# Loads and stores of a first block: where residual rows, quarters of a weight and split weight terms stand in one DMA queue

## The chip, the cores and the metric

The kernel runs on one core of a Trainium2 chip, as one launch. The metric is the device time of that launch in microseconds (us); lower is better.

## The reference

The input x has shape (4, 1024, 512), in float32. Two branches start from the same layer norm of x, and both are added to x:

```python
xn = layernorm(x)                                   # over the last axis, 512 wide

# time mix: 512 -> 704 -> 512
xx = concat([xn[:, 1:2], xn[:, :-1]], axis=1) - xn  # the row before, minus this row
k = (xn + xx * time_mix_k) @ Wk.T                   # (b, t, 704)
r = (xn + xx * time_mix_r) @ Wr.T
w = exp(-exp(time_decay))
state = state * w + relu(k_t)                       # a scan over t
a = layernorm((state * r) @ Wv.T) * ln_gamma + ln_beta

# FFN: 512 -> 2048 -> 512, rounded to float16 at three places
X = xn.astype(float16)
D = gelu(X @ W0.T + bias0).astype(float16)
E = (D @ W1.T + bias1).astype(float16)

out = x + a + E
```

## The kernel before

**Tiles.** The 4096 rows of x are worked in 8 blocks of 512 tokens (`TB`). A block is computed with channels on the partitions: 512 channels are 4 tiles of 128 (`NC`, index c), the 704 hidden units of the time mix are 5 full tiles and a half one (index h), the 2048 of the FFN are 16 tiles (`NN`, index n), and the 512 tokens of an output are 4 tiles of 128 (`NS`, index s). Index i is the block in the FFN, j = i + 1 the block whose time mix is under way, j2 = i + 2 the block whose rows are being fetched and normalized.

**Split weights.** Matmuls work on pairs of float32r tiles that sum to the float32 value. `split(hi, lo, raw)` makes such a pair: ACT casts the raw tile to the upper part (L165), then DVE subtracts to get the lower (L166). W0 comes in four quarters, *groups* g = 0 to 3, each of 512 hidden units, which serve the four chunks n = 4g to 4g + 3. A group is four raw tiles `w0raw_{g}_{c}` of 256 KB (loaded at L173), whose pairs `w0h`, `w0l` stay for the whole kernel. W1 is split chunk by chunk in block 0 (`w1raw_{n}`, loaded at L182; `w1_0_{n}` has two buffers), the pair is stored in DRAM as `w1d_{n}` (L193, 512 KB), and later blocks load it from there. The weights of k and r are split into three terms each (`split_kr`, tiles `wt_...`, six buffers under the tag `kr`), which are stored as `krd_...` (L223, three stores of 256 KB) for later blocks. Other parts of weights and inputs share a pool of 48 buffers.

**The chunk loop.** Before the loop, block 0's time mix projections are computed, groups 0 and 1 of W0 are loaded and split, chunks 0 and 1 of `up` are issued, and block 1's rows are loaded, normalized and transposed (`transposed`, 16 instructions of DVE at L284). Then each block runs 16 chunks. In chunk n, PE does

- `up(i, n + 2)`: 8 matmuls into a bank `pd` (L650), two for each c; ACT follows with gelu (L660, tile `d16`) and a copy to float32r (L665, tile `d`);
- `down(n)`: 8 matmuls that add to the four banks `pe` (L672), from `d` and the pair of W1;
- a *piece* of the time mix: for n = 0 to 3 `out_piece`, one s of the product with Wv (L578 and, at n = 1 and 3, L590), followed on DVE by a layer norm and by the addition of the residual rows (`residual`, L604, L610, L611); later pieces are the projections of block j.

What lies beside this is put into the lists `bg[n]` by `put(n, ...)` and issued at the end of chunk n: the mixing of block j's inputs (`mixed`), splits, the load of block j2's rows (`fetch_x`), its statistics and its transposes, and the load of the residual rows (`fetch_res`).

**Order.** Inside the loop the order on PE and on the DMA queue of SP is the order of the program (`manual_schedule`); ACT, DVE and POOL are ordered by a planner, which places each instruction by estimated costs and due times. Before the loop the planner orders SP too. Every engine and queue works in its order, so a DMA that has to wait for its source or its buffer holds up those behind it. All of the DMAs named here are issued on SP.

**Buffers that matter here.** A block's rows `x_{i}` and its residual rows `xres_{i}` are tiles of the tag "x", which has one buffer (`load_x`, four DMAs of 256 KB at L100). So `xres_0` can be fetched only after the last transpose of `x_1`, and `x_2` only after the last use of `xres_0`.

Of the kernel before, what the change touches and what calls it, by code (L numbers as in the profile page):

```python
# [11 lines left out]
F32 = mybir.dt.float32  # L12
# [10 lines left out]
def time_mix_and_gelu_ffn(  # L23
# [26 lines left out]
    nc = tc.nc  # L50
# [5 lines left out]
    NC = C // P  # L56
# [21 lines left out]
    def part(name, dtype=F32R, tag="q", bufs=48):  # L78
        return wide.tile([P, TB], dtype, tag=tag, name=name, bufs=bufs)
# [10 lines left out]
    def tokens_of(i, s):  # L90
        b, t0 = blocks[i]
        return b, slice(t0 + s * P, t0 + (s + 1) * P)

    def load_x(i, name, amid=lambda: None):
        xs = const.tile([P, NS, C], F32, tag="x", name=f"{name}_{i}")
        for s in range(NS):
            if s == NS // 2:
                amid()
            b, rows = tokens_of(i, s)
            nc.sync.dma_start(xs[:, s, :], x[b, rows, :])  # L100
        return xs
# [62 lines left out]
    def split(hi, lo, raw):  # L164
        nc.scalar.copy(hi, raw)  # L165
        nc.vector.tensor_sub(lo, raw, hi.bitcast(F32))  # L166

    G = TB // P
    w0 = {}

    def load_w0(g, c):
        raw = part(f"w0raw_{g}_{c}", F32)
        nc.sync.dma_start(raw, w0T[c * P : (c + 1) * P, g * TB : (g + 1) * TB])  # L173
        w0[c, g] = part(f"w0h_{c}_{g}"), part(f"w0l_{c}_{g}")
        split(*w0[c, g], raw)

    w1_dram = [dram.tile([P, 2, C], F32R, name=f"w1d_{n}") for n in range(NN)]
    w1_raw = {}

    def load_w1_raw(n):  # L180
        w1_raw[n] = part(f"w1raw_{n}", F32)
# [2 lines left out]
    def load_w1(i, n):  # L184
        if i == LAST and n >= NN - 2:
            parts = [part(f"w1_{i}_{n}_{p}") for p in range(2)]
            for p in range(2):
                nc.sync.dma_start(parts[p].bitcast(F32), w1_dram[n][:, p, :].bitcast(F32))
            return parts
        w1 = wide.tile([P, 2, C], F32R, tag="w1", name=f"w1_{i}_{n}", bufs=2)  # L190
        if i == 0:
            split(w1[:, 0, :], w1[:, 1, :], w1_raw.pop(n))
            nc.sync.dma_start(w1_dram[n].bitcast(F32), w1.bitcast(F32))  # L193
        else:
            nc.sync.dma_start(w1.bitcast(F32), w1_dram[n].bitcast(F32))
        return [w1[:, p, :] for p in range(2)]
# [15 lines left out]
    def split_kr(kind, h):  # L212
        raw = raw_w.pop((kind, h)).rearrange("p c k -> p (c k)")
        name = f"{kind}_{h}"
        u = truncated(raw, f"wu_{name}")
        d = temp(f"wd_{name}")
        nc.vector.tensor_sub(d, raw, u)
        terms = [part(f"wt_{name}_{p}", tag="kr", bufs=6) for p in range(3)]
        nc.scalar.copy(terms[0], u)
        nc.scalar.activation(terms[1], d, AF.Copy, scale=S)  # L220
        nc.vector.scalar_tensor_tensor(terms[2], d, -S, u, ALU.mult, ALU.add)
        for p in range(3):
            nc.sync.dma_start(kr_dram[kind, h][p].bitcast(F32), terms[p].bitcast(F32))  # L223

    def split_half():
        u = truncated(raw_half.rearrange("p two c k -> p (two c k)"), "half_u")
# [52 lines left out]
    def transposed(xn, first=0, end=(P // Q) ** 2):  # L279
        src = xn.rearrange("p s (c i a) -> p s c i a", c=NC, a=Q)  # L280
        dst = xnT[:, :, 1:].rearrange("p c (s j b) -> p s c j b", s=NS, b=Q)
        for k in range(first, end):
            j, i = divmod(k, P // Q)
            nc.vector.transpose(  # L284
                dst[i * Q : (i + 1) * Q, :, :, j, :],
                src[j * Q : (j + 1) * Q, :, :, i, :],
            )
# [285 lines left out]
    pos, zs, xres = {}, {}, {}  # L573
# [127 lines left out]
    for g in range(2):  # L701
        for c in range(NC):
            load_w0(g, c)
    for n in range(AHEAD):
        load_w1_raw(n)
    load_late_constants()
# [2 lines left out]
    norm_stats(1, x_now)  # L709
    norm_apply(1, x_now)  # L710
    transposed(x_now)
    behind.close()
    xres[0] = load_x(0, "xres")
    for n in range(AHEAD, AHEAD + 2):
        load_w1_raw(n)

# [2 lines left out]
    with tc.manual_schedule(engines={nc.tensor.engine, nc.sync.engine}):  # L719
        for i in range(len(blocks)):  # L720
            j, j2 = i + 1, i + 2
            tail = 4 if i == LAST else 0
            by_columns = range(NS // 2, NS) if tail else ()
            pieces, bg, pre = {}, defaultdict(list), defaultdict(list)

            def put(n, fn, *args):
                bg[n].append(lambda: fn(*args))

            for s in range(NS):
                pieces[s] = [out_piece, i, s]  # L730
            if j <= LAST:
                if i == 0:
                    order = [(0, h) for h in range(NF)] + [(1, h) for h in range(NF)]
                    for k, (kind, h) in enumerate(order):
                        pieces[4 + k + kind] = [(raw_k, raw_r)[kind], j, h]
                        put(5 + k, split_kr, kind, h)
                    pieces[9] = [
                        lambda j: raw_halves(j, [bank(f"pkr_{j}_{q}") for q in range(2)]), j
                    ]
                    put(13, split_half)  # L740
                    for c in range(NC):
                        put(c, mixed, j, c)
                        put(c, load_w0, 2, c)
                        put(6 + c, load_w0, 3, c)
                else:
                    order = [(0, h) for h in range(NF)] + [(1, h) for h in range(NF)]
                    for k, (kind, h) in enumerate(order):
                        pieces[4 + k + 2 * kind] = [three_pass, j, kind, h]

                        def fetch(kind, h):  # L750
                            ks[j, kind, h] = load_kr(j, kind, h)

                        put((2, 3)[k] if k < 2 else 2 + k + 2 * (k > 6), fetch, kind, h)
                    pieces[9] = [half_pass, j, 0]
                    pieces[10] = [half_pass, j, 1]
                    for c in range(1, NC):
                        put(c - 1, mixed, j, c)
                    put(4, split_xr, j, 0)
                    put(8, split_xr, j, 1)
                    put(9, split_xr, j, 2)  # L760
                    put(9, split_xr, j, 3)
            if j2 <= LAST:

                def fetch_x():
                    state["x"] = load_x(j2, "x")

                put(5, fetch_x)
                put(6, lambda: norm_stats(j2, state["x"]))
                put(7, lambda: norm_apply(j2, state["x"]))
                for n, ks_ in enumerate((0, 5, 10, 16)[:-1]):  # L770
                    end = (5, 10, 16)[n]
                    put((8 if i == 0 else 10) + n, lambda a, b: transposed(state["x"], a, b), ks_, end)
                put(13, mixed, j2, 0)
            if j <= LAST:

                def fetch_res():
                    xres[j] = load_x(j, "xres")

                put(14, fetch_res)

            pe = [ps_e.tile([P, C], F32, tag="pe", name=f"pe_{i}_{s}") for s in range(NS)]
            for n in range(NN):
                ahead = n + AHEAD
                if ahead == NN and j <= LAST:
                    xf = ffn_input(j)
                nxt = (i, ahead) if ahead < NN else (j, ahead - NN)
                gelu = up(*nxt) if nxt[0] <= LAST else None
                for follow in followers:
                    follow()
                followers = []  # L790
                if gelu:
                    d = gelu()
                if n == 0:
                    for s, e16 in enumerate(e16s):
                        finish(i - 1, s, e16)
                    e16s = []
                if n < NN - tail:
                    operands = waiting.pop(0)
                    for s in range(NS):
                        down(n, s, *operands, end=NN - tail if s in by_columns else NN)  # L800
                if gelu:
                    waiting.append((d, load_w1(*nxt)))
                if n in pieces:
                    fn, *args = pieces[n]
                    followers.append(fn(*args))
                if i == 0 and n + 4 < NN:
                    load_w1_raw(n + 4)
                for fn in bg[n]:
                    fn()
            if not tail:  # L810
                e16s = [rounded(i, s, pe[s]) for s in range(NS)]

# [56 lines left out]
```

## Time and profile before

| what | value |
|---|---|
| time, median of 3 runs | 931.48 us (931.17 to 932.77) |
| profiled execution, device time | 930.21 us |
| profiled execution, span of the trace | 928.1 us |
| mean granted TensorE clock in it | 0.989 |
| PE busy | 900.6 us (97% of the span) |
| DVE busy | 569.4 us (61%) |
| ACT busy | 340.6 us (37%) |
| POOL busy | 64.2 us (7%) |
| DMA, mean rate | 174 GB/s, 161.66 MB |

The profile records one execution. Its span runs from the first instruction to the last, and 2.1 us of its device time lie outside. Busy time is summed over an engine's instructions. In the timeline a row gives the start, the length, the engine (SPq is the queue of SP in the act of issuing DMAs), the line of the program, the operation, what it writes and reads, and in brackets the idle time ahead of it and what ended that. In the waits a row gives the instruction that waited, what released it, and then the total in us, the number of times and the longest. In the windows a row gives the stretch and its length, then the busy us of PE, PE's weight loads, DVE, ACT and POOL with the number of instructions, then the granted clock of PE as a share of full speed, the busy share of the DMA engines and the GB/s they moved.

Block 0 takes the first part of the span: its chunk loop begins at about 67 us, and the chunk n = 10 lies at about 142 to 160 us.

### The profile page before, as it was taken

Reading aid. Unit: us, or ns where it says so; the run is one execution under the profiler, and the core shown is the slowest. Engines: PE = TensorE matmul, PEld = TensorE weight load, DVE = VectorE, ACT = ScalarE, POOL = GpSimd, SP = SyncE. Lnnn points to the kernel's source line nnn. Section 1 sums busy time; section 2 is a strip of 40 time slices with the busy share of each in tenths; the row PEclk is TensorE's granted clock in tenths of the full one; section 3 lists DMA queues with packets and bytes.
Section 4 is the critical chain, followed back from the end, with each engine's and each line's share of the span. In section 5 each row is a group of like instructions: output and inputs, shape, how many; then the busy total and the mean of one; then the engine's idle time right before and its main releaser. Section 6 shows DMA issues by size and latency. Waiting matters only on the chain.

```text
span 928.1 us, 10514 instructions
## 1 busy us (share of the span) xinstructions
PE 900.6 (97%) x3664; PEld 651.4 (70%) x3664; DVE 569.4 (61%) x954; ACT 340.6 (37%) x578; POOL 64.2 (7%) x142
## 2 busy tenths in 40 slices
PE   8959995999999999999999999999999999999997
PEld 8435663665888668885788758886688857887586
DVE  5975588763586845966478735868459674423223
ACT  4442353531345223442345313442244523442132
POOL 1200000001100010001110001001100000000000
PEclk9989997999999999999999999999999999999999
DMA  9333374563646347462565536463474735655134
GB/s 264 133 125 134 124 253 159 216 227 135 229 153 230 114 168 242 157 228 102 178 231 167 185 136 217 157 223 129 156 245 151 241 103 168 196 161 190 69 116 156
DMA packets 75727, 161.66 MB, mean 174 GB/s; under 512 B 8959, under 2 KB 15132, under 8 KB 75676
## 3 DMA queue, kind: packets, MB, share of 16 engines
q1 hardware_dynamic: 75616, 160.99, 51.7%
q8 instruction: 29, 0.48, 0.2%
q14 instruction: 22, 0.18, 0.1%
q10 hardware_dynamic: 60, 0.02, 0.0%
HBM read 136.33 MB, written 24.64 MB: 173 GB/s over the span
## 4 chain that ended last, share of the span: by engine, by line
PE 91%; DVE 3%; DMA 2%; issue 1%; SPq 1%; ACT 1%; POOL 0%; DVEq 0%; ACTq 0%
PE pe L672 24%; PE pd L650 24%; PE po L578 15%; PE pa L524 12%; PE pb L325 6%; PE pr L325 3%; PE pk L325 2%; PE ph L552 2%; PE po L590 2%; DVE xnT L284 1%; DMA w0raw<-in_L_ffn_W 1%; PE idle L343 1%; DMA w<-w1d 1%; DMA x<-in_L_attn_x 0%; PE end L672 0%
## 5 line engine op out<-in xcount | busy, mean ns | idle before, releaser
L672 PE MATMUL pe<-w,d 128*128 128x512 f32 x1008 | 252.9, 393 | 11.4 <-ACT d L665 10.2
L672 PEld LDWEIGHTS pe<-w,d 128*128 128x128 f32 x1008 | 191.1, 190 | 53.1 <-ACT d L665 11.8
L650 PE MATMUL pd<-xf,w0h 128*128 128x512 f32 x512 | 212.5, 415 | 7.1 <-ACT w0h L165 7.1
L650 PE MATMUL pd<-xf,w0l 128*128 128x512 f32 x512 | 200.4, 391 | 2.4 <-DVE w0l L166 2.4
L660 ACT ACTIVATE d<-pd,late_sb 128x512 f16<-128x512 f32 x128 | 87.8, 686 | 268.1 <-PE pd L650 267.8
L578 PE MATMUL po<-wv_sb,g 128*128 128x512 f32 x320 | 142.6, 592 | 0.0
L650 PEld LDWEIGHTS pd<-xf,w0h 128*128 128x128 f32 x512 | 96.3, 188 | 47.5 <-issue 19.9
L650 PEld LDWEIGHTS pd<-xf,w0l 128*128 128x128 f32 x512 | 96.3, 188 | 28.0 <-issue 6.2
L578 PEld LDWEIGHTS po<-wv_sb,g 128*128 128x128 f32 x320 | 60.9, 190 | 63.8 <-issue 60.6
L260 DVE BATCH_NORM_STATS2 sty<-po 128x6 f32<-128x512 f32 x32 | 21.9, 683 | 124.4 <-PE po L590 124.4
L537 DVE SCALAR_TENSOR_TENSOR y<-pb,a 128x512 f32<-128x512 f32 x60 | 41.3, 689 | 91.8 <-PE pb L325 91.3
L665 ACT CAST d<-d 128x512 fp32r<-128x512 f16 x128 | 79.3, 620 | 3.6
L284 DVE STREAM_TRANSPOSE xnT<-x 32x512 f32<-32x512 f32 x112 | 78.7, 702 | 2.0
L536 ACT ACTIVATE a<-pa 128x512 f32<-128x512 f32 x60 | 35.9, 599 | 114.7 <-PE pa L524 114.7
L524 PE MATMUL pa<-hk,kr 128*128 128x512 f32 x120 | 46.7, 389 | 0.0
L524 PE MATMUL pa<-lk,kr 128*128 128x512 f32 x120 | 46.7, 389 | 0.0
L524 PE MATMUL pa<-hr,kr 128*128 128x512 f32 x120 | 46.7, 389 | 0.0
L524 PE MATMUL pa<-lr,kr 128*128 128x512 f32 x120 | 46.7, 389 | 0.0
L254 POOL TENSOR_SCALAR ry<-mvy 128x1 f32<-128x1 f32 x32 | 15.6, 487 | 423.8 <-DVE mvy L261 423.8
L325 PE MATMUL pk<-xk,wk 128*128 128x128 f32 (+1 forms) x152 | 38.6, 410 | 0.0
L325 PE MATMUL pr<-xr,wr 128*128 128x512 f32 x80 | 35.6, 592 | 0.0
L539 ACT ACTIVATE y<-y 128x512 f32<-128x512 f32 x30 | 19.0, 633 | 43.9 <-DVE y L537 43.9
(130 smaller groups left out, 1001.4 us busy)
## 6 DMA issues: line engine op xcount, KB each, us to landing
w<-w1d SPq DMA_DIRECT2D x110, 512.0 KB, 3.3
kr<-krd SPq DMA_DIRECT2D x180, 256.0 KB, 4.0
x<-in_L_attn_x SPq DMA_DIRECT2D x32, 256.0 KB, 5.0
xres<-in_L_attn_x SPq DMA_DIRECT2D x32, 256.0 KB, 4.4
w1d<-w SPq DMA_DIRECT2D x16, 512.0 KB, 2.9
krd<-wt SPq DMA_DIRECT2D x30, 256.0 KB, 3.6
out<-z SPq DMA_DIRECT2D x28, 256.0 KB, 2.5
w0raw<-in_L_ffn_W SPq DMA_DIRECT2D x16, 256.0 KB, 4.6
```

Source lines behind the costliest of these rows:

```text
L260: nc.vector.bn_stats(st6, src)
L284: nc.vector.transpose(dst[i * Q : (i + 1) * Q, :, :, j, :], src[j * Q : (j + 1) * Q, :, :, i, :],)
L325: return nc.tensor.matmul(dst, w[:, c, :], src, start=(c == 0), stop=(c == NC - 1))
L524: nc.tensor.matmul(pa, w[p][:, c, :], xs[j, c][p], start=(c == 0 and p == 0), stop=(c == NC - 1 and p == 1),)
L536: nc.scalar.activation(a, pa, AF.Copy, scale=1.0 + 1.0 / S)
L537: nc.vector.scalar_tensor_tensor(y, pb, -1.0 / S, a, ALU.mult, ALU.add)
L539: nc.scalar.activation(y, y, AF.Relu)
L578: nc.tensor.matmul(pos[s], gs[i, h][:, s * P : (s + 1) * P], wv_sb[:, h, :], start=(h == 0), stop=False,)
L650: nc.tensor.matmul(pd, w0[c, g][p][:, k * P : (k + 1) * P], xf[c], start=(c == 0 and p == 0), stop=(c == NC - 1 and p == 1),)
L660: nc.scalar.activation(d16, pd, AF.Gelu, bias=b0_sb[:, n : n + 1])
L665: nc.scalar.copy(d, d16)
L672: nc.tensor.matmul(pe[s] if sum_ is None else sum_, d[:, s * P : (s + 1) * P], w1[p][:, cols], start=(n == first and p == 0), stop=(n == e ...
```

## The change

Four things change, all of them in what runs before block 0's loop or within its 16 chunks; the blocks after it run the same instructions.

1. `xres[0] = load_x(0, "xres")` moves from before the loop into `bg[0]`, the end of chunk 0.
2. Group 2 of W0 (the third quarter) is loaded and split before the loop, right behind block 1's transposes in the program, rather than in chunks 0 to 3.
3. `load_w0` is divided into the load and `split_w0`. For group 3 (the last quarter), the loads go to the ends of chunks 4 to 7 and take buffers of the tag `kr`, which the terms of k and r use as well; the splits stay in chunks 6 to 9.
4. The stores of W1's pairs and of the terms of k and r are put in a list when their data is made, and `store_weights()` issues them at the end of the chunk, behind the loads that the chunk issues.

```diff
-    def load_w0(g, c):
-        raw = part(f"w0raw_{g}_{c}", F32)
+    w0_raw = {}
+
+    def load_w0(g, c, **home):
+        w0_raw[c, g] = raw = part(f"w0raw_{g}_{c}", F32, **home)
         nc.sync.dma_start(raw, w0T[c * P : (c + 1) * P, g * TB : (g + 1) * TB])
+
+    def split_w0(g, c):
         w0[c, g] = part(f"w0h_{c}_{g}"), part(f"w0l_{c}_{g}")
-        split(*w0[c, g], raw)
+        split(*w0[c, g], w0_raw.pop((c, g)))
...
+    stores = []
+
+    def store_weights():
+        while stores:
+            nc.sync.dma_start(*stores.pop(0))
...
             split(w1[:, 0, :], w1[:, 1, :], w1_raw.pop(n))
-            nc.sync.dma_start(w1_dram[n].bitcast(F32), w1.bitcast(F32))
+            stores.append((w1_dram[n].bitcast(F32), w1.bitcast(F32)))
...
         for p in range(3):
-            nc.sync.dma_start(kr_dram[kind, h][p].bitcast(F32), terms[p].bitcast(F32))
+            stores.append((kr_dram[kind, h][p].bitcast(F32), terms[p].bitcast(F32)))
...
     for g in range(2):
         for c in range(NC):
             load_w0(g, c)
+            split_w0(g, c)
...
     transposed(x_now)
+    for c in range(NC):
+        load_w0(2, c)
+        split_w0(2, c)
     behind.close()
-    xres[0] = load_x(0, "xres")
...
+            if i == 0:
+
+                def first_res():
+                    xres[0] = load_x(0, "xres")
+
+                put(0, first_res)
...
                     for c in range(NC):
                         put(c, mixed, j, c)
-                        put(c, load_w0, 2, c)
-                        put(6 + c, load_w0, 3, c)
+                        put(4 + c, partial(load_w0, tag="kr", bufs=6), 3, c)
+                        put(6 + c, split_w0, 3, c)
...
                 for fn in bg[n]:
                     fn()
+                store_weights()
```

## The prediction

> **What bounds the kernel now.** I read the page's busy shares first (PE 97% busy, 900.6 of 928.1 us), then the waits of PE, then the timeline of its two long waits, then the windows for the clock. PE lacks 27.5 us, and three waits hold most of it:
>
> ```profile
> PE pe L672 <- ACT d L665: 10.2, 1, 10.2
> PE pd L650 <- ACT w0h L165: 7.1, 2, 6.0
> PE pd L650 <- DVE w0l L166: 2.4, 1, 2.4
> ```
>
> All three lie in block 0, which the change edits. The others are under 2 us each.
>
> **Stall 1, 57.27 to 67.47.** The timeline shows a chain that starts on the SP queue:
>
> ```profile
> 54.78 1.28 SPq L100 DMA_DIRECT2D xres<-in_L_attn_x  x3
> 56.10 0.43 SPq L173 DMA_DIRECT2D w0raw<-in_L_ffn_W  x1
> 61.28 0.62 ACT L165 CAST w0h<-w0raw 128x512 fp32r<-128x512 f32 x1 [3.74 <-DMA w0raw<-in_L_ffn_W]
> 65.71 0.69 ACT L660 ACTIVATE d<-pd,late_sb 128x512 f16<-128x512 f32 x1
> 67.47 3.78 PE L672 MATMUL pe<-w,d 128*128 128x512 f32 x8 [10.21 <-ACT d L665]
> ```
>
> xres_0 shares its one buffer with x_1, so SP holds it until x_1's last transpose (L284) at 54.75. The last load of group 1, w0raw_1_3, stands behind it. ACT works in order: its cast of that tile waits 3.74 us, and kr, relu, the gelu table, gelu and d follow, 6.2 us of mere succession up to the first down().
>
> **Stall 2, about 146 to 158**, inside up(0,12), the first product with group 3:
>
> ```profile
> 148.28 0.32 SPq L193 DMA_DIRECT2D w1d<-w  x1
> 149.01 0.69 DVE L166 TENSOR_TENSOR w0l<-w0raw,w0h 128x512 fp32r<-128x512 f32 x1
> 149.12 1.87 SPq L223 DMA_DIRECT2D krd<-wt  x3
> 151.10 0.66 SPq L173 DMA_DIRECT2D w0raw<-in_L_ffn_W  x1
> 155.76 0.62 ACT L165 CAST w0h<-w0raw 128x512 fp32r<-128x512 f32 x1 [2.19 <-DMA w0raw<-in_L_ffn_W]
> 156.43 0.80 PE L650 MATMUL pd<-xf,w0h 128*128 128x512 f32 x1 [5.96 <-ACT w0h L165]
> ```
>
> The last raw tile stands on SP behind a store waiting for DVE's lower part of w1_0_11 (ends 148.25) and behind three krd stores: issued 151.1, landed 155.7. Undisturbed, up(0,12) would end at 146.33; it ends at 157.95: 11.6 us lost, the waits of 1.16, 2.4 and 6.0 and matmuls at half clock between.
>
> **Clock.** In the windows (busy us by engine, PEclk, DMA share, GB/s), what follows each stall still runs at half rate:
>
> ```profile
> 61.13:67.40 6.27, 0.00 (x0) 0.00 (x0) 4.62 (x8) 5.22 (x8) 0.57 (x1) 0.50 0.35 135
> 67.40:71.37 3.97, 3.90 (x9) 3.13 (x10) 2.41 (x5) 2.09 (x5) 0.00 (x0) 0.50 0.65 264
> 156.40:160.12 3.72, 3.69 (x8) 2.67 (x9) 3.65 (x7) 2.63 (x5) 0.00 (x0) 0.50 0.00 0
> 130.00:152.00 22.00, 16.93 (x79) 9.53 (x77) 21.34 (x33) 8.46 (x15) 0.06 (x1) 0.95 0.63 210
> ```
>
> Half rate costs 1.95 us in the first (3.9 of work at half) and 1.07 in the second (a down() of 2.89 instead of 1.82). The last row counts later: ahead of stall 2 DVE is 97% busy. Losses in all: 10.2 + 1.95 + 11.6 + 1.07 = 24.8 us.
>
> **The Trainium skill.** "TensorE: Matmul & The Clock Gate", Part 1, What's actually happening: after at least one idle window of about 3.4 us the array runs at half clock, and at full after a busy one; the window runs freely. The trace agrees: half from 61.13, 3.86 us after the last matmul, to 71.37, 3.90 after the first. The same page, Architectural detail: ACT and DVE are strict FIFO; here ACT stood 3.74 us at a cast while its next input was ready. "DMA: Bandwidth & Descriptors", Anatomy of one DMA: a semaphore wait is taken on the issuing sequencer, not by the DMA engines; here w0raw_1_3 issued only after xres had its buffer.
>
> **The change part by part.** The counts of PE and POOL instructions stay, and all weight transfers stay on SP.
>
> *xres_0 moved into chunk 0.* SP is idle from 28.1, so w0raw_1_3 issues at once there and lands long before its cast. That goes from 61.28 to about 57.5, where ACT comes from the previous cast: the 3.74 us go, nothing else of the chain. First down() at 67.47 - 3.74 = 63.73, a gap of 6.46, still long enough for half clock; the 1.95 stay, with 0.15 added for the different place in a window: 2.1. xres_0's four DMAs then pass through SP at 59 to 61, landing by 65 (4.4 us to landing on the page); their first reader (L611) comes after 84, so they cost nothing. Without that 19 us the cost would be the chain itself. Gain 3.74 - 0.15 = **3.6**.
>
> *Group 2 ahead of the FFN.* Its four loads, 1 MB, fall into 28 to 54, where DMA is 21% busy (1% in 40 to 50). Four casts of 0.62 and four subtractions of 0.69 move from chunks 0 to 3 to ACT's and DVE's order before, between and after the transposes of x_1. DVE was the busier one, 25.8 of 28 us in 26:54, so they partly fill the gap and can push. They were in chunks where up(0,8) is still 30 us off. Bounds: -0.5 (less crowding in chunk 1) to +2.8 (four DVE splits all before d_0_0). I take 0: the cast that gates gelu hangs on w0raw_1_3, and DVE's share in the gap was 4.62 of 6.27 with slack between.
>
> *What becomes late next.* In the changed kernel's instruction order on ACT, the cast of w1_0_2 no longer comes right after the first down() (71.29 before) but after d_0_4, and DVE's lower part behind z work of the first pair (L604, L610, L611). PE, from 63.73: down 3.7 at half clock, po_0 4.5, up 1.84, down 1.82, po_1 with its halves 5.3, up(0,4) to about 82.95. Then gelu at 83.04, d 83.76, w1's cast 84.28 to 84.90, lower part 85.66 to 86.34, so that the second matmul of down(2) starts at 86.4 rather than 83.2: **3.2 lost** (2.4 if the subtraction goes first, 4.0 if one more z operation precedes it). ACT then waits at w1_0_4 for the landing of w1_0_2's store (about 89.5); the next gelu's input is there only at 94, so this is hidden by 4 us.
>
> *Group 3 two chunks ahead in kr's buffers.* Loads 0 and 1 go at 98 to 111; load 2 must wait until a krd store has landed (about 120), load 3 until a subtraction frees its buffer (130 to 133). It lands by 138, 17 us earlier than now. Stall 2 so loses its DMA part, and what remains is DVE: x_2's load is issued at about 110 rather than 116.85, as it stands behind less on SP, its sixteen transposes of 0.70 end about 5 us earlier, and the last subtraction w0l_3_3 lands at 148.4 to 149.3 (behind the terms of kr_0_4 and w1_0_11) instead of 157.1. With PE arriving 0.5 earlier, up(0,12) would end at 145.8 and ends at 149.0: **3.2 lost** instead of 11.6, and the 1.07 of half clock goes if PE is not idle for a whole window.
>
> The casts of terms borrow from the same six buffers, so ACT may wait for stores: 3.6 us to landing plus 0.6 each for issue. A gelu has about 7 us (one chunk) before down() needs it, so this is 0 while the wait is under that; bounds 0 to 2 per chunk in chunks 6 to 12.
>
> *Stores behind loads.* Same 46 stores, moved back within their chunk by at most a w1 load, four x loads and a w0 load (0.4, 2.3 and 0.7 us of issue). Their readers come only in block 1, over 50 us later. Waiting at the end rather than in the middle, they hold up the next chunk's loads alone, which are two to four chunks early. Zero; bounds -0.5 to +0.5.
>
> Sum: losses after 6.46 + 2.1 + 3.2 + 3.2 = 15.0, so 24.8 - 15.0 = **9.8 us gained**, without new half clock. Both short gaps are just under or about a window with one or two matmuls inside. Before stall 2 a window with roughly 0.5 us of PE work out of 3.4 dropped the clock, one with 2.7 did not; where the limit lies between is not shown. A drop costs 1.7 (half of a window) to 2.5; one in the first gap is passed on, since DVE's later work hangs on PE's through z and the terms. The profiled execution of 930.21 would become 920.4 without a drop; it lies 1.27 below the median of 931.48, so against the median 921.7, with one drop about 923.9, with two 926.2.
>
> **Rivals.**
> 1. *Both gaps drop the clock*: gain 5.3, 926. For: the gaps are as long as a window. Against: matmuls in them.
> 2. *DVE holds stall 2 as it is.* If x_2's transposes aren't earlier, DVE, 97% busy until 152, gives w0l_3_3 at about 153 (the present 157.1 less the 4 that its own load no longer costs), half clock again: up(0,12) ends at 153.7 instead of 157.95, and 4.2 is the whole gain: 927.3.
> 3. *Slower: kr's six buffers.* If terms wait for landed stores in each chunk from 6 to 12, ACT stands 3.6 + 0.6 us while holding the next gelu; where that exceeds the chunk's slack by 1.8 in seven chunks, 12.6 are lost, total 934. It decides once the sum passes 9.8. For: w0raw_3 takes up to four of six. Against: ACT is 37% busy, and a term's chunk is 7.1 us long.
> 4. *The change doesn't do what it says*: the load of group 1 still waits for another buffer. Up to 190 us SP waits only for the subtraction (L193) and for x's buffer (L100), which speaks against it; then stall 1 stays, and 9.8 - 3.6 = 6.2 is left: 925.3.
>
> **Numbers.** Short stalls with at most one drop: 0.62, 921.7 to 923.9; I predict 923.5, nearer the one drop, which I hold for likelier than none. Two drops (rival 1) 0.15; rival 2: 0.09; rival 4: 0.03; slower 0.08; losses that happen to cancel 0.03. Low end 919 from the lower bounds (2.4, one gap less); high end 929 takes in rivals 1, 2 and 4. 0.2% (1.9 us) is about what can be told from no change here.
>
> **What would show it.** Right: w0raw_1_3 issued near 28; first down() near 63.7; a new wait of 1 to 3 us of L672 on w1's cast or subtraction near 83 to 86; w0raw_3_3 issued before 135; the longest wait of L650 under 4 us near 146. Wrong: any wait above 4 us in chunks 5 to 12, ACT idle on krd landings with PE idle beside it, or stall 1 still near 10 us.

## The result, and the profile after

Over seven runs the changed kernel took 925.10 us (923.71 to 928.82), the kernel before 931.53, 6.4 us more. The ratio of the means is 0.9937, with a 95% interval of 0.9919 to 0.9955. The profiled execution was the slowest of the seven, 928.82 us with a span of 926.9, so I read a second trace of the same kernel beside it (label after_again: 924.44 us, span 922.6).

In the code of the changed kernel the lines of the loop stand nine further down: `up` is L659, `down` L681, gelu L669, the copy to d L674, the transposes L293. The waits of PE in the first trace (total, times, longest):

```profile
PE pe L681 <- ACT d L674: 6.5, 1, 6.5
PE small L409 <- issue: 3.1, 1, 3.1
PE pd L659 <- ACT w0h L165: 2.4, 1, 2.4
PE pe L681 <- ACT w L165: 2.0, 1, 2.0
PE pd L659 <- DVE w0l L166: 1.5, 1, 1.5
PE pe L681 <- DVE w L166: 1.0, 1, 1.0
```

The first wait was 10.2. The second belongs to the start of the kernel (2.0 before, so that the prediction's "under 2 us each" for the other waits is just off). The third and fifth together were 9.5, and the two on `w`, 3.0 in all, are new: they stand at `down(2)`. The page's line of busy times,

```profile
PE 904.3 (98%) x3664; PEld 653.3 (70%) x3664; DVE 569.0 (61%) x954; ACT 339.3 (37%) x578; POOL 65.6 (7%) x142
```

shows PE busier than before by 3.7 us with the same 3664 matmuls. That is no extra work: matmuls at half clock last longer, and this execution had more of them. Its windows, in the same columns as before:

```profile
6.00:9.00 3.00, 0.20 (x1) 0.13 (x1) 0.43 (x3) 0.54 (x3) 0.00 (x0) 1.00 0.67 227
9.00:16.00 7.00, 6.87 (x31) 6.28 (x32) 3.55 (x15) 3.51 (x11) 1.59 (x4) 0.51 0.92 253
87.60:94.40 6.80, 5.83 (x11) 3.49 (x11) 5.23 (x9) 0.78 (x2) 0.00 (x0) 0.50 0.65 231
155.80:159.20 3.40, 3.40 (x10) 2.66 (x9) 2.58 (x5) 2.02 (x4) 0.00 (x0) 0.50 1.03 357
```

PE was nearly idle from 6 to 9 us, while the first rows came in, and ran at half rate up to 16. In the trace of the kernel before, it was busy for 1.61 of these 3 us. That kernel, too, was slow at the start, for a shorter time. Its records of the clock begin only at 13.3 us, and a window ahead of that prints 1.00, but matmuls of the same shape took nearly twice as long there (18 in 3.94 us, behind it 24 in 2.96):

```profile
9.66 3.94 PE L325 MATMUL pk<-xk,wk 128*128 128x128 f32 x18
13.87 2.96 PE L325 MATMUL pk<-xk,wk 128*128 128x128 f32 x24
```

With the later start, `up(0, 1)` ended 1.9 us later than before, at 59.16. The other two rows follow the new gap at `down(2)` and the rest of stall 2. The second trace has a milder start and no drop after `down(2)`. Its timeline of PE's waits in block 0 is the one to hold against the prediction:

```profile
63.47 3.74 PE L681 MATMUL pe<-w,d 128*128 128x512 f32 x8 [6.44 <-ACT d L674]
84.52 0.49 PE L681 MATMUL pe<-w,d 128*128 128x512 f32 x1 [2.01 <-ACT w L165]
86.10 1.89 PE L681 MATMUL pe<-w,d 128*128 128x512 f32 x7 [1.08 <-DVE w L166]
148.72 0.62 PE L659 MATMUL pd<-xf,w0h 128*128 128x512 f32 x1 [3.06 <-ACT w0h L165]
150.69 0.80 PE L659 MATMUL pd<-xf,w0l 128*128 128x512 f32 x1 [1.35 <-DVE w0l L166]
```

Predicted were 63.73 for the first, 84.9 and 86.4 for the two at `down(2)`, and 149.0 for the end of `up(0, 12)`, which came at about 151.5. Other signs that it had named are there as well: the last raw tile of group 1 was issued by 28.4, that of group 3 at 131.76, and no wait of PE in chunks 5 to 12 is above 4 us.

### The profile page after: what moved, and what is told of

Same layout as the page of the kernel before. It is cut to its first block, busy times and chain, and to the rows that moved or that the text cites. A ratio compares the mean times of both kernels' runs of the same rounds, so it can differ in the third digit from the quotient of the medians.

```text
span 926.9 us, 10511 instructions
## 1 busy us (share of the span) xinstructions
PE 904.3 (98%) x3664; PEld 653.3 (70%) x3664; DVE 569.0 (61%) x954; ACT 339.3 (37%) x578; POOL 65.6 (7%) x142
## 4 chain that ended last, share of the span: by engine, by line
PE 86%; DVE 5%; DMA 5%; issue 1%; SPq 1%; ACT 1%; POOL 0%; DVEq 0%; ACTq 0%
PE pe L681 24%; PE pd L659 23%; PE po L587 15%; PE pa L533 12%; PE pb L334 6%; PE ph L561 2%; PE pr L334 2%; PE po L599 2%; DVE xnT L293 2%; DMA krd<-wt 1%; DMA wr<-in_L_attn_Wr 1%; DMA x<-in_L_attn_x 1%; DMA wk<-in_L_attn_Wk 1%; DMA wv_sb<-in_L_attn_Wv 1%; DVE w0l L166 1%
## 5 line engine op out<-in xcount | busy, mean ns | idle before, releaser
L681 PE MATMUL pe<-w,d 128*128 128x512 f32 x1008 | 255.4, 396 | 10.6 <-ACT d L674 6.5
L681 PEld LDWEIGHTS pe<-w,d 128*128 128x128 f32 x1008 | 191.9, 191 | 53.6 <-ACT d L674 8.0
L659 PE MATMUL pd<-xf,w0h 128*128 128x512 f32 x512 | 212.1, 414 | 2.4 <-ACT w0h L165 2.4
L659 PE MATMUL pd<-xf,w0l 128*128 128x512 f32 x512 | 199.9, 390 | 1.5 <-DVE w0l L166 1.5
L669 ACT ACTIVATE d<-pd,late_sb 128x512 f16<-128x512 f32 x128 | 87.8, 686 | 284.0 <-PE pd L659 283.8
L659 PEld LDWEIGHTS pd<-xf,w0h 128*128 128x128 f32 x512 | 96.1, 188 | 42.3 <-issue 20.1
L659 PEld LDWEIGHTS pd<-xf,w0l 128*128 128x128 f32 x512 | 96.2, 188 | 26.8 <-issue 6.2
L674 ACT CAST d<-d 128x512 fp32r<-128x512 f16 x128 | 79.4, 620 | 3.7
L293 DVE STREAM_TRANSPOSE xnT<-x 32x512 f32<-32x512 f32 x112 | 78.7, 702 | 2.0
```

Source lines behind the costliest of these rows:

```text
L293: nc.vector.transpose(dst[i * Q : (i + 1) * Q, :, :, j, :], src[j * Q : (j + 1) * Q, :, :, i, :],)
L659: nc.tensor.matmul(pd, w0[c, g][p][:, k * P : (k + 1) * P], xf[c], start=(c == 0 and p == 0), stop=(c == NC - 1 and p == 1),)
L669: nc.scalar.activation(d16, pd, AF.Gelu, bias=b0_sb[:, n : n + 1])
L674: nc.scalar.copy(d, d16)
L681: nc.tensor.matmul(pe[s] if sum_ is None else sum_, d[:, s * P : (s + 1) * P], w1[p][:, cols], start=(n == first and p == 0), stop=(n == e ...
```

## The experiments

Each time stands against the kernel before on the same chip: 932.23 in the first group, 931.74 in the second, 932.08 in the third.

### First group: the changed kernel with single orders mended

**The changed kernel again (after_again).** No edit.

> The changed kernel once more, for a second trace and for its time beside the others of this chip. Theory A: in the first trace of it, up(0,1) ended 1.9 us later than before and the clock was at half from 9 to 16 us; up to there both kernels issue the same DMAs in the same order, so this is chance: it will be missing here, or show in the kernel before as well, and the time is about 925. Theory B: it belongs to the change, is there again, and costs 2 us each time.

Measured: 924.37 us, ratio 0.9919 (0.9895 to 0.9942). From 6 to 9 us PE was busy for 0.98, and the mean clock from 9 to 16 was 0.76: one slow window instead of two, and `up(0, 1)` ended at 57.0. The traces of three single-part kernels below, which issue the same work up to 20 us as the kernel before, also have half clock in 9 to 16 (a mean of 0.78, 0.77 and 0.54), and in the last of them, last_only, `up(0, 1)` ended at 58.2. So theory A: the late start is chance and not the change's. It also means that times of single traces differ by up to 2 us from their start alone.

**The pair of `w1_0_2` first (pair_first).** Planner edges put ACT's cast and DVE's subtraction of `w1_0_2` ahead of what follows `up(0, 4)`:

```diff
+            state["w1", n] = split(w1[:, 0, :], w1[:, 1, :], w1_raw.pop(n))
...
+                with ExitStack() as behind_w1:
+                    if nxt == (0, 4):
+                        for part_ in state["w1", 2]:
+                            behind_w1.enter_context(tc.issue_after(part_.ins))
+                    for follow in followers:
+                        follow()
...
+                    if gelu:
+                        d = gelu()
```

> The changed kernel, with only the order at chunk 2 undone: ACT's cast and DVE's subtraction of w1_0_2 come ahead of gelu of chunk 4 and of the first pair's z work. Theory A (the waits at down(2) are planner order, and what they cost, 3.0 us of waits and up to 3.4 of half clock, goes on to the end): no wait of L681 near 85, and 919 to 922. Theory B (DVE sets the end of up(0,12) anyway, so that time won at chunk 2 is given back there): the waits near 85 go, those near 153 grow by as much, 924.5 to 925.5.

Measured: 921.38, ratio 0.9884 (0.9866 to 0.9902). PE's waits in it:

```profile
PE pe L681 <- ACT d L674: 6.5, 1, 6.5
PE pd L659 <- ACT w0h L165: 2.5, 1, 2.5
PE pd L659 <- DVE w0l L166: 1.5, 1, 1.5
```

The waits on `w` are gone, those in `up(0, 12)` are no longer than in the changed kernel (4.0, against 3.9 and 4.4 in its two traces), and the time is 3.0 lower: theory A. From the end of `up(0, 1)` to the end of the span, which leaves the start out, its trace took 862.1, those of the changed kernel 865.5 and 867.8. So what was lost at `down(2)` went on to the end.

**The splits of group 3 a chunk earlier (split_first).**

```diff
-                        put(6 + c, split_w0, 3, c)
+                        put(5 + c, split_w0, 3, c)
```

> The changed kernel, with each split of group 3 put one chunk earlier (chunks 5 to 8 instead of 6 to 9; the loads stay). Theory A: what is left at up(0,12) is DVE's and ACT's order, not their amount of work; the waits near 153 (2.4 and 1.5) and a half clock of 1.7 go, the waits at chunk 2 stay: 920 to 922. Theory B: DVE is full, so an earlier split makes another instruction late and a wait of the same 3 to 4 us appears elsewhere between 100 and 160: 924 to 926.

Measured: 922.92, ratio 0.9898 (0.9871 to 0.9924), with a wide spread: three runs at 918.83 to 921.40 with a mean clock of 0.993 or 0.994, three at 924.44 to 925.33 with 0.987. The median lies between the ranges of the two theories. The trace is of the 924.44 one. In it the wait on `w0h` is gone, 1.6 on `w0l` is left, and no new wait stands between 100 and 160. So the rest of stall 2 shrinks as theory A says. There is half clock from 7.3 at the start, from 85.8 after `down(2)`, and from 911.8 in the last block. Which of these the three faster runs lack is not shown, so the median says little by itself.

**Both orders (both_first).**

> Both of these edits in one kernel. Theory A: they add; only the wait of about 6.5 at the first down() is left in block 0: 916 to 918.5. Theory B: they don't add since DVE sets the pace: within 1 us of the better of the two.

Measured: 915.49, ratio 0.9832 (0.9811 to 0.9853). In block 0 two waits are left:

```profile
PE pe L681 <- ACT d L674: 6.5, 1, 6.5
PE pd L659 <- DVE w0l L166: 1.6, 1, 1.6
```

8.9 below the changed kernel: the two add. The medians of the single edits give 3.0 + 1.5, but with the spread of split_first it isn't shown that they more than add. In this trace no gap of block 0 after the first drops the clock (1.00 from 140 to 146); two of the five runs, at 917.53 and 918.41, have a lower mean clock. DVE did the same work (569.0 us busy, and 14.67 of 15 from 120 to 135), so it was not the limit by its amount of work. It was the order in which its work stood.

### Second group: one part of the change alone, on the kernel before

**Residual rows (residual_only).**

```diff
-    xres[0] = load_x(0, "xres")
...
+                put(0, first_res)
```

> The kernel before, with only xres_0's load moved into chunk 0. Theory A (the prediction's): the cast of w0raw_1_3 no longer waits, the first wait of L672 falls from 10.2 to about 6.5 and the second stall stays as it is: 3 to 4 us below before, 928. Theory B: the second stall ends when its load has landed, whatever PE does ahead of it, so the gain is given back: within 1 us of before.

Measured: 927.49, ratio 0.9951 (0.9936 to 0.9966). The first wait fell to 6.48, the second stall's three waits are 1.98, 2.38 and 5.93, much as before. Theory A.

**Third quarter (third_only).**

```diff
     transposed(x_now)
+    for c in range(NC):
+        load_w0(2, c)
...
-                        put(c, load_w0, 2, c)
```

In the kernel before, `load_w0` holds the split too.

> The kernel before, with only group 2 loaded and split ahead of the loop. Theory A (the prediction took 0): both stalls stay, within 1.5 us of before. Theory B: the four splits crowd ACT and DVE in the first stall and lengthen it by up to 2.8: up to 3 us above before. Theory C: fewer loads and splits in chunks 0 to 3 take a little off: 1 us below.

Measured: 932.43 over 21 runs, ratio 1.0005 (0.9997 to 1.0014): nothing, as in theory A. The first wait is 10.4, the second stall's are 2.1, 2.2 and 6.0.

**Last quarter (last_only).**

```diff
-                        put(6 + c, load_w0, 3, c)
+                        put(c, split_w0, 2, c)
+                        put(4 + c, partial(load_w0, tag="kr", bufs=6), 3, c)
+                        put(6 + c, split_w0, 3, c)
```

The load and the split are two functions here, as in the changed kernel; group 2 stays where it was.

> The kernel before, with only group 3's loads two chunks ahead in kr's buffers. Theory A (the prediction's): the wait on the DMA of w0raw_3_3 goes, a wait of 3 to 4 for DVE's or ACT's order is left in up(0,12): 5 to 8 us below before. Theory B: with the stores in place ahead of it the load of w0raw_3_3 is still late: less than 2 us below before.

Measured: 928.14, ratio 0.9963 (0.9948 to 0.9977), 3.6 less: between the two theories. Its timeline shows why:

```profile
119.39 1.97 SPq L100 DMA_DIRECT2D x<-in_L_attn_x  x4
151.65 2.85 DVE L288 STREAM_TRANSPOSE xnT<-x 32x512 f32<-32x512 f32 x4
154.53 0.69 DVE L166 TENSOR_TENSOR w0l<-w0raw,w0h 128x512 fp32r<-128x512 f32 x1
155.28 0.79 PE L654 MATMUL pd<-xf,w0l 128*128 128x512 f32 x1 [4.34 <-DVE w0l L166]
```

No DMA is late any more, but x_2 is fetched at 119.39 (116.85 before; 1.5 of the difference is that the first `down` of this trace is so much later), behind the stores of terms, and four of its transposes stand ahead of the last subtraction. The DMA wait has turned into a DVE wait.

**Stores behind loads (stores_only).**

```diff
-            nc.sync.dma_start(w1_dram[n].bitcast(F32), w1.bitcast(F32))
+            stores.append((w1_dram[n].bitcast(F32), w1.bitcast(F32)))
...
-            nc.sync.dma_start(kr_dram[kind, h][p].bitcast(F32), terms[p].bitcast(F32))
+            stores.append((kr_dram[kind, h][p].bitcast(F32), terms[p].bitcast(F32)))
...
                 for fn in bg[n]:
                     fn()
+                store_weights()
```

This moves the stores of W1's pairs as well as those of terms.

> The kernel before, with only the stores of terms put behind each chunk's loads. Theory A (the prediction's): 0, within 0.5 us of before, as no reader of the stores is near. Theory B: w0raw_3_3's load is one of the loads that they stood ahead of, 2.8 us in the second stall (148.28 to 151.1), and x_2's load too, so the stall shortens: 3 to 5 us below before.

Measured: 926.31, ratio 0.9942 (0.9925 to 0.9959), 5.4 less: theory B, and by the medians the largest of the four parts, though its interval overlaps that of the residual rows. In the kernel before, x_2's load stood behind a store of a pair of W1, which waited for DVE until 114.1, and behind three stores of terms:

```profile
114.10 0.33 SPq L193 DMA_DIRECT2D w1d<-w  x1
114.95 1.86 SPq L223 DMA_DIRECT2D krd<-wt  x3
116.85 2.32 SPq L100 DMA_DIRECT2D x<-in_L_attn_x  x4
149.74 2.14 DVE L284 STREAM_TRANSPOSE xnT<-x 32x512 f32<-32x512 f32 x3
```

In this kernel's timeline

```profile
109.28 1.89 SPq L100 DMA_DIRECT2D x<-in_L_attn_x  x4
143.91 0.71 DVE L289 STREAM_TRANSPOSE xnT<-x 32x512 f32<-32x512 f32 x1
146.98 0.33 SPq L173 DMA_DIRECT2D w0raw<-in_L_ffn_W  x1
150.69 0.79 PE L655 MATMUL pd<-xf,w0h 128*128 128x512 f32 x1 [4.55 <-ACT w0h L165]
```

x_2's load is 7.6 earlier than before, the last transpose is over at 144.6 (151.9 before), and the last raw tile is issued at 146.98 instead of 151.1. One wait of 4.55 is left of 9.5. How much of this comes from x_2's rows and how much from the raw tile is not separated.

### Third group: the change without one part, and a combination

**Without the third quarter (without_third).** `put(c, load_w0, 2, c)` and its split back in chunks 0 to 3.

> The changed kernel with group 2 back in chunks 0 to 3 (its loads and splits as before). Theory A (the late pair of w1_0_2 is how the planner's order comes out when group 2 stands ahead of the loop and the stores behind the loads, both together): no wait of L681 near 85, up(0,12) as in the changed kernel, so the time is that of the kernel with the pair first, 920 to 922.5. Theory B (group 2's early loads are needed): a wait on w0h or w0l of group 2 appears in chunks 5 to 7, and the time is 925 or more.

Measured: 921.38, ratio 0.9880 (0.9862 to 0.9899), with no wait between 64 and 145 us; those in `up(0, 12)` are 2.77 and 1.47. Theory A: the part that does nothing alone costs 3 to 4 us in company (924.37 and 925.10 against 921.38). Nothing of group 2 was late without it.

**Without the stores' move (without_stores).** The two `stores.append(...)` back to `nc.sync.dma_start(...)`.

> The changed kernel with the stores back in their places. Theory A (the stores ahead of x_2's load are what keeps DVE's transposes late): x_2's load is issued after 114 again, w0l_3_3 stands behind the transposes on DVE, the waits in up(0,12) sum to 5 to 7; no wait near 85; 923 to 926. Theory B (the stores don't matter, as the prediction had it): waits in up(0,12) of 4 as in the changed kernel, no wait near 85: 920 to 922.5.

Measured: 924.58, ratio 0.9915 (0.9899 to 0.9931). x_2's load is at 114.41, and the waits in `up(0, 12)` are

```profile
PE pd L659 <- DVE w0l L166: 4.3, 1, 4.3
PE pd L659 <- ACT w0h L165: 2.4, 1, 2.4
```

6.7 in all; at `down(2)` there is none. Theory A. The stores' move gains at `up(0, 12)` and, together with group 2 ahead of the loop, loses at `down(2)`; so taking it away leaves the time of the changed kernel (924.37) as it is.

**A combination (combined).** Both orders of the first group mended, and two more. The core of what is new:

```diff
+        if n == 0:
+            first_gelu = state["gelu"]
+            with tc.issue_after(first_gelu.ins):
+                halves()
+            with tc.issue_after(first_gelu.ins):
+                for c in (2, 3):
+                    split_w0(1, c)
...
+                    def mixed_behind(j, c):
+                        with tc.issue_after(first_gelu.ins):
+                            mixed(j, c)
...
+                        if i == 0 and b == 16:
+                            behind_w0.enter_context(tc.issue_after(state["w0"].ins))
                         transposed(state["x"], a, b)
```

Here `halves` is what ACT and DVE do after the half head's matmuls in block 0, and `state["w0"]` is the last subtraction of group 3.

> The kernel with both waits' orders mended, and two more orders: on ACT, the first gelu comes ahead of everything that waits for DVE (the casts of x_1's transposed rows, the half head's sums and relu, and the casts of group 1's last two tiles), and on DVE the last six transposes of x_2 come behind the last subtraction of group 3. Theory A (what is left of stall 1 is ACT's order, not its work): the first down() starts within 1 us of the end of up(0,1), no half clock there, and the 6.5 of wait, the half clock of 2 to 3.5 and the 1.6 at up(0,12) all go: 905 to 908. Theory B (DVE and ACT are full at that point, so that the work put behind gelu makes po_1 or the casts for block 1 late): 3 to 6 of it come back as waits in chunks 1 to 3: 909 to 913.

Measured: 910.05, ratio 0.9758 (0.9741 to 0.9776), 14 to 15 below the changed kernel. Where stall 1 was, and at the start of block 1:

```profile
54.00:66.00 12.00, 12.00 (x46) 8.23 (x45) 11.64 (x19) 8.65 (x16) 0.56 (x1) 1.00 0.60 207
176.52 2.97 PE L683 MATMUL pe<-w,d 128*128 128x512 f32 x8 [2.31 <-ACT d L669]
```

PE is without a gap from 54 to 66, at full clock, and no wait is left in block 0's loop. ACT and DVE were busy as long as in the changed kernel (338.1 and 568.6 us over the span, against 339.3 and 569.0); only their order differs. A new wait of 2.31 opens at the first `down` of block 1, where casts of the next inputs, which wait for DVE, stand ahead of a gelu, and one slow window follows it at 178.1. The median lies in the range of theory B, but its waits in chunks 1 to 3 did not come: stall 1 went as theory A says, and a wait that neither had named took its place. Without the 2.31 and up to 1.7 for half a window, 906 would be left, by estimate.

## Why the prediction was right, and where it was not

**The total.** 923.5 was predicted, 925.1 measured, in the range and near the case of one drop (923.9). The waits that the prediction leaves in block 0 sum to 6.46 + 3.2 + 3.2 = 12.9; those in the two traces sum to 13.4 and 13.9. So the total held because what the changed kernel would still wait for was right. Which part of the change buys it was wrong for two parts, and there the errors cancel in the sum. The number of drops is in part luck: behind stall 1, the first trace has one after `down(2)` and one at `up(0, 12)`, the second only the latter.

**Residual rows: right.** Predicted gain 3.6, measured alone 4.2 (931.74 - 927.49). The first `down` started at 63.47 in the second trace, 63.73 predicted, and stayed at half clock.

**Group 2: right alone, wrong in company.** I took 0, and alone it is 0. The 3.2 lost at `down(2)` I had nearly right (waits of 3.0 and 3.1), but I put them down to ACT's order as such. The run without the third quarter has no such wait, and neither has the run without the stores' move: the late pair of `w1_0_2` needs both parts, so it belongs in their account. Whether these two suffice, and why the planner orders so, is not shown.

**Group 3: the gain was given to the wrong part.** The loads of group 3 went where they were predicted (98.19, 108.42, 120.59 and 131.76 in the second trace). The step that failed is "Stores behind loads. ... Zero". I had written under group 3 that x_2's load comes at about 110 "as it stands behind less on SP", and that is the stores' doing. Counted from the first `down`, x_2's load is issued after 49.4 us in the kernel before, 50.4 with group 3 moved alone and 50.2 without the stores' move, but after 41.5 with the stores moved alone and 42.5 in the run without the third quarter. In the changed kernel it is 45.8 and 49.0 in the two traces, where the gap at `down(2)`, in the first trace with a drop of the clock behind it, comes in between. I argued zero from the stores' readers, which are indeed far off, and left out the loads that the stores stood ahead of, though my own lines of stall 2 show three stores of terms ahead of the last raw tile. Alone, the stores are worth 5.4 and group 3 is worth 3.6. Both cut the same stall: its waits were 9.5 before, 6.8 with group 3 alone, 4.6 with the stores alone and 4.2 with both and the residual rows. In company, taking the stores' move away does leave the time as it is, as a zero would have it, but by a gain and a loss that cancel: luck.

**The rest of stall 2: 3.2 predicted, 4.4 measured** (3.06 and 1.35 in the second trace, 3.9 in the first). The last subtraction ended at 150.6, not at 148.4 to 149.3: ACT's cast of `w0raw_3_3` stood behind a term of kr_0_4, and DVE's subtraction behind that of `w1_0_11`, each a little later than in my walk. Rival 2 rested on x_2's transposes not coming earlier; they did (the last ended at 148.2 in the second trace, at 151.9 before). That DVE, as a resource, holds the stall is refuted by the run with both orders, in which only 1.6 of it is left with the same work.

**The clock: the size of a drop was too small.** I allowed 1.7 to 2.5 for one. In the first trace the drop after `down(2)` lasted two windows of 3.41 us, and 5.83 us of PE's time in it cost 2.9. At `up(0, 12)`, the gap dropped the clock in every trace of a kernel whose waits there summed to 3.9 or more, so that I had its chance too low; at `down(2)` two traces of three show a drop.

**The sum of the parts.** Alone, residual rows, last quarter and stores give 4.2 + 3.6 + 5.4 = 13.2. Together, which is the run without the third quarter, they give 932.08 - 921.38 = 10.7. The difference is no larger than the intervals allow; that the last two share a stall is read from the waits above. Group 2 then takes back 3 to 4.

**Rivals 3 and 4** did not come: no wait of PE between 90 and 140 in any trace, and stall 1 was cut as planned. In the second trace, ACT waited for landed stores of terms for 0.4 us in all. That chance of a slower kernel had no mechanism behind it that the runs show.

## What to carry to other kernels

When a store moves back in a queue, its price is not read from its readers alone but from every load that it stood ahead of, and from what those loads release. When a wait on a DMA is removed, look for what is next in order on the engines behind it: here the same stall turned from a DMA wait into a wait on DVE, and only an order of two or three instructions was left to mend. An engine that is 97% busy ahead of a stall is not yet the bound; ask whether the one instruction that is waited for could have stood earlier in its order.

## What the runs showed of the hardware

The granted clock in the records is full or half, and it changes on a grid of 3.41 us: stretches at half clock that ended within the span lasted 3.41, 6.83, 10.24 or 13.65 us. So each of these windows can be held against PE's work in the window before it. From 20 us on and up to the last block, in all 13 traces, a window at full clock in which PE was busy for 1.58 us or less was followed by half clock (1.40 in the first trace of the changed kernel, 1.41 in split_first, 1.58 in combined), and one with 1.83 or more by full clock (1.83 in both_first, 1.84 and 1.91 in the second trace of the changed kernel). The first two lines are of combined, the third is of both_first, which stayed at full clock:

```profile
174.69:178.10 3.41, 1.58 (x6) 0.89 (x6) 3.41 (x6) 1.94 (x4) 0.00 (x0) 1.00 0.35 137
178.10:181.51 3.41, 3.41 (x7) 1.83 (x6) 3.12 (x6) 0.00 (x0) 0.00 (x0) 0.50 0.54 204
142.30:145.71 3.41, 1.83 (x8) 1.43 (x8) 3.19 (x10) 2.14 (x4) 1.04 (x3) 1.00 0.00 0
```

So a gap of 2.3 us, well under a window, can already cost half clock. In the last block the same limit doesn't hold: a window with 2.23 us busy was followed by half clock in third_only, one with 2.33 by full clock in the kernel before. The Trainium skill, "TensorE: Matmul & The Clock Gate", Part 1, What's actually happening, speaks of at least one idle window; here a window with PE busy for 46% of it did it too, and the measurement decides.

In five of the 13 traces the records of the clock begin only at 13 to 13.6 us, and a window ahead of that prints 1.00 although the matmuls there run at half rate, as the two lines of the kernel before show. A mean granted clock leaves that stretch out.

That the windows lie differently against a gap in each run would account for part of the spread of 6.5 us in one kernel (split_first, 918.83 to 925.33, with mean clocks of 0.994 and 0.987): in the first trace of the changed kernel the drop after `down(2)` cost 2.9. One trace of split_first doesn't show more.
